# Graph attention's query stores and the first tile's query load on ACT's DMA queue

## The chip, the cores and the metric

The kernel runs on one core of a Trainium2 chip. The metric is the device time of one execution in microseconds (us); of several executions the median is given. PE (TensorE) is the matrix engine, DVE (VectorE), ACT (ScalarE) and POOL (GpSimd) are the others, and SP (SyncE) only issues transfers. SP and ACT each have a DMA queue of their own, in which an engine's transfers stand in program order among its other instructions; POOL issues the indirect transfers. "Tile" is used for a block of 128 nodes.

## The reference

Two layers of a graph network over 1250 nodes with 512 channels and 40000 edges. Each layer adds a graph part, a mixing part and a feed-forward part. The change concerns the graph part of the first layer, an attention in which every edge carries one score per head (8 heads of 64 channels):

```python
xn = _layernorm(x, axis=-1)
x = x + _L0_gnn_ref(xn, edge_index, edge_attr_8, ...) + _L0_mix_ref(xn[None], ...)[0]
...
def _L0_gnn_ref(x, edge_index, att_bias, Wq, bq, Wk, bk, Wv, bv, Wo, bo, ...):
    src = edge_index[0]
    dst = edge_index[1]
    z = _layernorm(x, ln_att_g, ln_att_b)
    q = (z @ Wq.T + bq).reshape(n, H, D)
    k = (z @ Wk.T + bk).reshape(n, H, D)
    v = (z @ Wv.T + bv).reshape(n, H, D)
    s = jnp.einsum('ehd,ehd->eh', q[src], k[dst]) / np.sqrt(D) + att_bias
    m = jax.ops.segment_max(s, src, num_segments=n)
    p = jnp.exp(s - m[src])
    denom = jax.ops.segment_sum(p, src, num_segments=n)
    alpha = p / jnp.where(denom[src] == 0, 1.0, denom[src])
    agg = jax.ops.segment_sum(alpha[:, :, None] * v[dst], src, num_segments=n)
    att = agg.reshape(n, C) @ Wo.T + bo
    x = x + att
    ...
```

After it come the feed-forward part of this layer, then the second layer (a graph convolution, a second mixing part, and a product-key feed-forward).

## The kernel before

The 1250 nodes are padded to 1280: ten tiles of 128. The sparse attention is computed as a dense one. First the 40000 edges are turned into a dense table `adj` in device memory, with a row for each pair (source, destination) and nine columns: eight sums of exp(bias) and a count of edges. Then, for each tile of 128 source nodes, the kernel loads that tile's 128 x 1280 x 9 slab of the table, forms the scores of these nodes against all nodes, takes exp, multiplies by the slab, and multiplies by the values. Nodes without an edge between them have weight 0.

**Edges.** `scatter_edges` (L303) is a generator that handles six columns of edges at a step. A step loads keys (`kr`, L311, on SP's queue apart from the first), compares them on DVE (L325, L335) to merge edges with equal keys, sums their weights on PE (L317), and has POOL add rows into `adj` with an indirect transfer (L351). There are 313 of these, 128 rows each. Other stages call `pump(n)` to run n steps in between, so that the edges are worked off beside the mixing part and the projections.

**Projections** (L605 to L640). `zT` is the normalised, transposed input. For three chunks of columns (512, 512, 256) and for the four blocks m of 128 channels, PE multiplies by Wk and by Wq into PSUM tiles `mm`, of which there are three (`ps_mm`, L75). ACT adds the bias: keys to `kT` in SBUF (L628), queries to `qs` (L632), of which there are three. The queries then go to `q_d` in device memory (L633, twelve stores, on SP's queue). After that, for ten tiles, PE multiplies by Wv (L637) and DVE adds the bias and keeps the values as `gva` (L638). A last `pump` empties the generator.

**Attention** (L645 to L806). The pools of the edges and of the projections are closed before it, so its tiles lie in space that those had. `load_tile(t)` (L654) issues two loads on SP's queue: the slab (L657, 5.9 MB), with added dependencies on the last two batches of scatters, so that all edges are in; and `q`, the queries of this tile's 128 nodes for all channels (L661, 256 KB). `load_tile(0)` is called first; the load of tile t+1 is called within tile t. `count` (L664) has ACT copy the slab's column of counts (`cnt`, L667) and stores it; `mark` (L674) makes DVE's mask `none` of it; `score` (L677) multiplies q by kT on PE (L683); `maxima` (L687) adds the mask on DVE and finds the largest score; then follow exp (L705), the product with the slab (L712), transposes (L722, L723) and the product with the values (L732).

**Order.** Inside the attention loop the order on PE, DVE and ACT is the one written out by hand (`tc.manual_schedule`, L774). Everything before it, the projections and `load_tile(0)`, and all of SP's queue, is ordered by the framework's scheduler when the kernel is built: it puts each engine's instructions into one fixed sequence and gives each the waits that its data and its space need. On the chip each engine then goes through its sequence. In the sequence that SP has here, the loads of q for tiles 0 and 1 come after the ninth query store, then come the last three query stores, and then the slabs of tiles 0 and 1.

Of the kernel before, what the change touches and what calls it, by code (L numbers as in the profile page):

```python
# [22 lines left out]
P = 128  # L23
# [43 lines left out]
def tile_gps_layers(ctx: ExitStack, tc: tile.TileContext, a, out):  # L67
    nc = tc.nc
# [6 lines left out]
    def ps_mm(shape=(P, 512), name="mm"):  # L75
        return psum.tile(list(shape), F32, tag="mm", bufs=3, name=name)
# [4 lines left out]
    def ps_tr(shape=(P, 512), name="tr"):  # L81
        return psum.tile(list(shape), F32, tag="tr", bufs=2, name=name)
# [34 lines left out]
    def col(name, j=0, n=1, p0=0, p1=P):  # L117
        c0 = COLS[name][0] + j
        return cols[p0:p1, c0:c0 + n]

    def rows_bc(pool, src, n, width=C, name="rows", eng=nc.sync):
        t = pool.tile([P, n, width], F32, name=name)
        eng.dma_start(t.rearrange("p r c -> p (r c)"),
                          bass.AP(tensor=src.tensor, offset=src.offset, ap=[[0, P], [1, n * width]]))
        return t

    def load_w(pool, name, kc, n, tag="w", bufs=None, eng=nc.sync):
        t = pool.tile([P, kc, n], F32, tag=tag, name=name, bufs=bufs)
        eng.dma_start(t, a[name].rearrange("(c p) o -> p c o", p=P))
        return t  # L130
# [16 lines left out]
    def norm_stats(pool, x_t, eps, name):  # L147

        st = pool.tile([P, 6], F32, tag="ln_st", name=name + "st")
        nc.vector.bn_stats(st, x_t)  # L150
        mv = pool.tile([P, 2], F32, tag="ln_mv", name=name + "mv")
        nc.vector.bn_aggr(mv, st)
        return mv[:, 0:1], rsqrt(pool, mv[:, 1:2], [P, 1], eps, name)
# [27 lines left out]
    def node_mm(ps, xT, t, w, rows=P):  # L181

        mm(ps[:rows], [(xT[:, c, t * P:t * P + rows], w[:, c, :]) for c in range(xT.shape[1])])
# [7 lines left out]
    def chan_mm(ps, w, m, xT, c0, cn):  # L191

        mm(ps, [(w[:, c, m * P:(m + 1) * P], xT[:, c, c0:c0 + cn]) for c in range(xT.shape[1])])
# [5 lines left out]
    q_d = dram.tile([P, KC, NP], F32, name="q_d")  # L199
# [63 lines left out]
    for c0 in range(0, EC, P):  # L263
        cn = min(P, EC - c0)
# [131 lines left out]
    def pump(n):  # L396
        for _ in range(n):
            next(edges, None)
# [206 lines left out]
    with tc.tile_pool(name="gqkv", bufs=2) as pq:  # L605
        gbv = rows_bc(pq, a["gnn_rows"][0:1], 1, name="gbv")
        wk = load_w(pq, "gnn_WkT", KC, C, bufs=3)
        wq = load_w(pq, "gnn_WqT", KC, C, bufs=3)
        wv = load_w(pq, "gnn_WvT", KC, C, bufs=3)
        zT = pq.tile([P, KC, NP], F32, name="zT", bufs=1)  # L610
        for t in range(NT):
            z = pq.tile([P, C], F32, tag="z", name="z")
            m, r = norm_stats(pq, xn[:, t, :], 1e-5, "lnz")
            b = pq.tile([P, 1], F32, tag="lnzb", name="lnzb")
            nc.vector.tensor_scalar(b, m, r, -1.0, op0=OP.mult, op1=OP.mult)
            nc.scalar.activation(z, xn[:, t, :], AF.Identity, scale=r, bias=b)
            ps = ps_tr((P, KC, P))
            for c in range(KC):
                nc.tensor.transpose(ps[:, c, :], z[:, c * P:(c + 1) * P], ident)
            for c in range(KC):  # L620
                nc.scalar.activation(zT[:, c, t * P:(t + 1) * P], ps[:, c, :], AF.Identity,
                                     scale=col("att_g", c), bias=col("att_b", c))
            nc.scalar.dma_start(xb_d[t * P:(t + 1) * P, :], xn[:, t, :])
        for c0, cn in CHUNKS:
            for m in range(KC):
                ps = ps_mm()
                chan_mm(ps[:, :cn], wk, m, zT, c0, cn)
                nc.scalar.activation(kT[:, m, c0:c0 + cn], ps[:, :cn], AF.Identity, bias=col("gnn_bk", m))  # L628
                ps = ps_mm()
                chan_mm(ps[:, :cn], wq, m, zT, c0, cn)  # L630
                qs = pq.tile([P, 512], F32, tag="qs", name="qs", bufs=3)
                nc.scalar.activation(qs[:, :cn], ps[:, :cn], AF.Identity, bias=col("gnn_bq", m))  # L632
                nc.sync.dma_start(q_d[:, m, c0:c0 + cn], qs[:, :cn])  # L633
                pump(1)
        for t in range(NT):
            ps = ps_mm()
            node_mm(ps, zT, t, wv)  # L637
            nc.vector.tensor_tensor(va[:, t, :], ps, gbv[:, 0, :], op=OP.add)  # L638
            pump(1)
        pump(EC)  # L640
# [5 lines left out]
    with (tc.tile_pool(name="gslab", bufs=2) as pslab, tc.tile_pool(name="gatt", bufs=1) as pa,  # L646
# [7 lines left out]
        def load_tile(t):  # L654

            sl = pslab.tile([P, NP, CH], F32, tag="slab", name="slab")
            ld = nc.sync.dma_start(sl.rearrange("p d c -> p (d c)"), adj_v[t * P:(t + 1) * P, :])  # L657
            for x in scattered[-2] + scattered[-1]:
                tc.add_manual_dep(ld.ins, x.ins.name, SYNC, reason="all edges are in")
            q = pw.tile([P, KC, P], F32, tag="q", name="q")  # L660
            nc.sync.dma_start(q, q_d[:, :, t * P:(t + 1) * P])  # L661
            tiles[t] = [sl, q]

        def count(t):  # L664
# [105 lines left out]
        def stage(i, back):  # L770
            return steps[i - back] if 0 <= i - back < n else None

        load_tile(0)
        with tc.manual_schedule(engines={nc.tensor.engine, nc.vector.engine, nc.scalar.engine}):  # L774
            mark(0, count(0))
            score(*steps[0])
            for i in range(n + 4):
                now, last, turned, gone, done = (stage(i, b) for b in range(5))
                nxt = stage(i, -1)
                if now:  # L780
                    maxima(*now)
                    if now[1] == 0 and now[0] + 1 < NT:
                        load_tile(now[0] + 1)
                if done and done[1] == KC - 1:
                    divide(done[0])
                if turned:
                    turn(*turned, 1)
                    av = values(*turned)
                if nxt:
                    score(*nxt)  # L790
                if now:
                    exponentials(*now)
                    if now[1] == KC - 1 and now[0] + 1 < NT:
                        cnt = count(now[0] + 1)
                if turned:
                    keep(*turned, av)
                if last:
                    weigh(*last)
                    turn(*last, 0)
                if now and now[1] == KC - 1 and now[0] + 1 < NT:  # L800
                    mark(now[0] + 1, cnt)
                if last and last[1] == KC - 1:
                    divisors(last[0])
                if gone and gone[1] == KC - 1:
                    spread_divisors(gone[0])
# [1195 lines left out]
```

## Time and profile before

| | us |
|---|---|
| median of 3 runs | 2412.15 (2410.34 to 2412.55) |
| the profiled execution | 2407.95 |
| its span, first to last instruction | 2406.0 |
| POOL's scatters (L351), first to last start | 194.3 to 787.3 |
| query projections (L632), first to last start | 666.4 to 737.5 |
| query stores (L633, SP's queue), first to last issue | 667.1 to 792.9 |
| loads of q (L661, SP's queue), first to last issue | 790.3 to 1089.4 |
| loads of the slabs (L657), first to last issue | 795.6 to 1108.4 |
| first copy of counts (L667), ACT | starts 812.3 |
| attention's scores (L683), first to last start | 794.2 to 1160.1 |

PE is busy for 1978.7 us of the span (82%), DVE for 1510.5 (63%), ACT for 809.2 (34%) and POOL for 695.8 (29%). These shares are means over stages with different limits. Times in views of the trace count from the span's start. An entry such as `ACT L632 ... [2.79 <-PE even L317]` says that ACT was idle for 2.79 us before this work, and that the idle time ended with PE's work on the tile `even` at L317. `PEclk` is the clock that was granted to PE, as a share of full speed.

### The profile page before, as it was taken

What the parts mean: (1) busy time and instruction counts of PE and PEld (TensorE: products, weight loads), DVE (VectorE), ACT (ScalarE), POOL (GpSimd) and SP (SyncE); (2) the same over time, 40 slices, a digit from 0 to 9 for tenths busy, and PEclk for the clock granted to TensorE, in tenths of its full rate; (3) what the DMA queues carried; (4) which work ended last, traced back from release to release, by engine and by line L of the source; (5) the groups of instructions that cost most, each with busy time, mean ns of one, the idle gap of its engine ahead of it and who ended that gap; (6) DMA issues with size and microseconds to landing.
All of it is one profiled execution on the core that took longest, in us unless ns stands there. A gap on an engine that the chain in (4) does not pass through costs nothing.

```text
span 2406.0 us, 29781 instructions
## 1 busy us (share of the span) xinstructions
PE 1978.7 (82%) x10588; PEld 1178.0 (49%) x10588; DVE 1510.5 (63%) x4838; ACT 809.2 (34%) x1529; POOL 695.8 (29%) x448
## 2 busy tenths in 40 slices
PE   0767698885498499999899999999999999978943
PEld 0335475552244266666544546667445445555521
DVE  3716958879961399999651446655222142589997
ACT  0100011110230277677441156665111132244653
POOL 2006888888888100000000000000000000036665
PEclk9987698986599699999999999999899999989975
DMA  9998565434542665665431200000300101000000
GB/s 352 367 418 237 111 127 113 86 61 88 136 72 10 238 224 186 232 217 193 139 119 35 68 3 1 1 1 29 136 27 27 35 7 64 22 22 10 10 9 17
DMA packets 134385, 255.79 MB, mean 106 GB/s; under 512 B 51805, under 2 KB 90134, under 8 KB 132572
## 3 DMA queue, kind: packets, MB, share of 16 engines
q1 hardware_dynamic: 81840, 233.85, 26.3%
q0 software_dynamic: 46512, 8.02, 7.0%
q10 hardware_dynamic: 5884, 12.03, 1.4%
q8 instruction: 83, 1.36, 0.2%
q14 instruction: 66, 0.54, 0.1%
HBM read 161.05 MB, written 92.80 MB: 106 GB/s over the span
## 4 chain that ended last, share of the span: by engine, by line
PE 46%; DVE 12%; ACT 6%; DMA 1%; issue 1%; SPq 0%; POOL 0%; ACTq 0%; DVEq 0%
PE mm L179 21%; PE one L732 4%; PE sc L683 3%; ACT wT L723 3%; PE ag L1385 2%; PE sc L1064 2%; PE one L722 2%; PE av L1118 2%; PE one L1105 2%; DVE sc L1745 2%; DVE ix L1686 1%; DVE ix L1695 1%; DVE rest L1698 1%; DVE v L1692 1%; DVE v L1694 1%
## 5 line engine op out<-in xcount | busy, mean ns | idle before, releaser
L351 POOL DMA_INDIRECT adj<-tot,idx x313 | 499.0, 1594 | 276.0 <-DMA kr<-key_d 180.5
L712 DVE SCALAR_TENSOR_TENSOR ex<-ex,slab 128x1280 f32<-128x1280 f32 x80 | 197.3, 2510 | 0.2 <-issue 0.2
L325 DVE SCALAR_TENSOR_TENSOR eq<-kr,key,upto 128x128 bf16<-128x128 f32 (+2 forms) x313 | 145.0, 474 | 66.6 <-DMA kr<-key_d 41.0
L1316 DVE SCALAR_TENSOR_TENSOR X<-mm,gate,X 128x512 f32<-128x512 f32 x80 | 60.0, 750 | 199.1 <-PE mm L179 199.0
L335 DVE TENSOR_SCALAR_CACHE_REDUCE eqx<-kr,key 128x384 bf16<-128x384 f32 (+1 forms) x312 | 175.3, 598 | 0.0
L1254 POOL MEMSET padded<- 128x128 f32 x3 | 0.5, 205 | 541.0 <-DVE faT L1139 541.0
L722 PE MATMUL one<-ident,ex 128*128 128x128 f32 x800 | 126.2, 286 | 25.2 <-ACT wT L723 19.9
L723 ACT COPY wT<-one 128x512 f32<-128x512 f32 (+1 forms) x240 | 116.1, 517 | 90.2 <-PE one L722 85.5
L179 PE MATMUL mm<-w,hT 128*128 128x512 f32 (+1 forms) x320 | 143.9, 601 | 0.0
L179 PE MATMUL mm<-faT,w 128*128 128x512 f32 (+1 forms) x384 | 141.8, 523 | 0.7 <-ACT bs L1138 0.7
L683 PE MATMUL sc<-kT,q 64*128 64x512 f32 (+1 forms) x480 | 103.7, 556 | 42.0 <-DMA q<-q_d 22.4
L693 DVE CUSTOM_DVE_ANT_0 ex<-sc,none 128x1280 f32<-128x1280 f32 x80 | 115.8, 1486 | 11.3 <-PE sc L683 10.0
L722 PEld LDWEIGHTS one<-ident,ex 128*128 128x128 f32 x800 | 84.5, 141 | 68.4 <-ACT wT L723 48.8
L1078 DVE CUSTOM_DVE_ANT_0 ex<-sc,cmask 128x512 f32<-128x512 f32 (+3 forms) x144 | 72.9, 560 | 69.2 <-PE sc L1064 69.1
L317 PEld LDWEIGHTS <-eq 128*128 128x128 bf16 x625 | 42.9, 102 | 133.6 <-DVE eq L325 88.7
L179 PEld LDWEIGHTS mm<-faT,w 128*128 128x128 f32 x384 | 74.6, 195 | 67.4 <-issue 66.1
L705 ACT ACTIVATE ex<-ex,low 128x1280 f32<-128x1280 f32 x80 | 104.7, 1360 | 6.0 <-DVE low L698 6.0
L669 POOL DMA_DIRECT2D deg_d<-cnt x10 | 8.5, 846 | 338.9 <-ACT attT L739 312.6
L732 PE MATMUL one<-wT,gva 128*64 128x128 f32 x1600 | 101.3, 284 | 3.4 <-ACT wT L723 1.5
L1310 ACT ACTIVATE hT<-mm,cols 128x512 f32<-128x512 f32 (+1 forms) x48 | 29.0, 608 | 218.4 <-PE mm L179 218.4
L732 PEld LDWEIGHTS one<-wT,gva 128*64 128x64 f32 x1600 | 91.6, 143 | 13.4 <-ACT wT L723 13.4
L179 PEld LDWEIGHTS mm<-w,hT 128*128 128x128 f32 (+1 forms) x320 | 60.8, 191 | 75.5 <-issue 75.5
(493 smaller groups left out, 4094.2 us busy)
## 6 DMA issues: line engine op xcount, KB each, us to landing
adj<-zrow SPq DMA_DIRECT2D x4, 14400.0 KB
slab<-adj SPq DMA_DIRECT2D x10, 5760.0 KB
kr<-key_d SPq DMA_DIRECT2D x50, 576.0 KB
cnt_d<-cnt SPq DMA_DIRECT2D x10, 640.0 KB
deg_d<-cnt POOLq DMA_DIRECT2D x10, 640.0 KB
adjT<-cnt_d SPq DMA_DIRECT2D x5, 1280.0 KB
adj<-tot,idx POOLq DMA_INDIRECT x313
fw<-in_L_ffn_W SPq DMA_DIRECT2D x8, 512.0 KB
```

Of the source, the lines that this page charges most:

```text
L179: nc.tensor.matmul(ps, lhsT=l, rhs=r, start=i == 0, stop=i == len(pairs) - 1)
L325: nc.vector.scalar_tensor_tensor(eq[:, :n], kr[:, k0 * P:k0 * P + n], key[:, c0 + c:c0 + c + 1], upto[:, B - 1 - c:, :].rearrange("p c x - ...
L335: nc.vector.tensor_scalar(eq[:, :n * P], kr[:, k0 * P:(k0 + n) * P], key[:, c0 + c:c0 + c + 1], None, op0=OP.is_equal, op1=OP.add, accum_o ...
L351: st = nc.gpsimd.indirect_dma_start(out=adj, out_offset=bass.IndirectOffsetOnAxis(ap=idx[:, c:c + 1], axis=0), in_=tot[:, c, :], in_offset ...
L683: nc.tensor.matmul(sc[e][:, d0:d0 + dn], lhsT=q[half(e), m, :], rhs=kT[half(e), m, d0:d0 + dn], start=True, stop=True)
L693: nc.vector.tensor_tensor_reduce(out=ex, in0=sc[e][:, :NP], in1=none, scale=-0.125, scalar=-LOWEST, op0=OP.add, op1=OP.min, accum_out=low[ ...
L705: nc.scalar.activation(exs[e], exs[e], AF.Exp, bias=low[:, e:e + 1], scale=-1.0)
L712: nc.vector.scalar_tensor_tensor(exs[e], exs[e], 1.0, sl[:, :, hd], op0=OP.mult, op1=OP.mult, accum_out=den[:, hd:hd + 1])
L722: nc.tensor.transpose(ps[:, k, :], weights[t, m][e][:, (d0 + k) * P:(d0 + k + 1) * P], ident)
L723: nc.scalar.copy(wT[:, d0:d0 + dn, :], ps[:, :dn])
L732: nc.tensor.matmul(av[half(e), 0, :], lhsT=va[:, d, hd * D:(hd + 1) * D], rhs=turned[e][:, d, :], start=d == 0, stop=d == NT - 1)
L1078: nc.vector.tensor_tensor_reduce(out=exs[e][:, d0:d0 + dn], in0=sc[k][e][:, :dn], in1=cmask[:, NP - n + d0:NP - n + d0 + dn], scale=-0.125 ...
```

## The change

The twelve stores of the queries are issued from ACT in place of SP. Of the ten loads of q, the one for tile 0 is issued from ACT, and the other nine from SP as before. What is stored and loaded stays as it was, and so do the tiles and their numbers of buffers.

```diff
@@ -630,7 +630,7 @@
                 chan_mm(ps[:, :cn], wq, m, zT, c0, cn)
                 qs = pq.tile([P, 512], F32, tag="qs", name="qs", bufs=3)
                 nc.scalar.activation(qs[:, :cn], ps[:, :cn], AF.Identity, bias=col("gnn_bq", m))
-                nc.sync.dma_start(q_d[:, m, c0:c0 + cn], qs[:, :cn])
+                nc.scalar.dma_start(q_d[:, m, c0:c0 + cn], qs[:, :cn])
                 pump(1)
@@ -658,7 +658,9 @@
             q = pw.tile([P, KC, P], F32, tag="q", name="q")
-            nc.sync.dma_start(q, q_d[:, :, t * P:(t + 1) * P])
+
+            queue = nc.sync if t else nc.scalar
+            queue.dma_start(q, q_d[:, :, t * P:(t + 1) * P])
             tiles[t] = [sl, q]
```

## The prediction

> **What bounds the kernel now.** I read the stage around the change. First came the order of time of SP's queue, because both moved transfers stand on it now.
>
> ```profile
> 723.27 4.60 SPq L633 DMA_DIRECT2D q_d<-qs  x2
> 790.34 1.29 SPq L661 DMA_DIRECT2D q<-q_d  x2
> 791.74 1.50 SPq L633 DMA_DIRECT2D q_d<-qs  x3
> 795.60 0.80 SPq L657 DMA_DIRECT2D slab<-adj  x2
> ```
>
> Columns: start, length, engine, line, tiles. SP stops after the ninth of twelve query stores at 727.9 and issues nothing until 790.34. What holds it is the load of q for tiles 0 and 1, which the scheduler put ahead of the last three stores. The chain that ended last, in order of time, shows what ends that wait and what follows:
>
> ```profile
> 787.28 2.93 DMA adj<-tot,idx
> 790.34 0.62 SPq L661
> ...
> 792.87 2.59 DMA q_d<-qs
> 795.60 16.62 DMA slab<-adj
> 812.32 2.46 ACT cnt L667
> 814.80 0.84 DVE none L675
> ```
>
> The q load is freed by the landing of the last edge scatter (787.28 + 2.93 = 790.21), not by its own data: its buffer lies where the edge tiles were. Then come three late stores, their landing, and the slab. So 5.3 us of the chain (790.34 to 795.60) belong to the transfers that the change moves. Next, the order of time of PE, ACT and DVE, for what runs while POOL scatters:
>
> ```profile
> 730.37 1.89 PE L179 MATMUL mm<-zT,gnn_WkT 128*128 128x256 f32 x8
> 732.09 1.89 PE L179 MATMUL mm<-zT,gnn_WqT 128*128 128x256 f32 x8
> 733.82 1.89 PE L179 MATMUL mm<-zT,gnn_WkT 128*128 128x256 f32 x8
> 735.54 1.89 PE L179 MATMUL mm<-zT,gnn_WqT 128*128 128x256 f32 x8
> 737.27 34.50 PE L179 MATMUL mm<-gnn_WvT,zT 128*128 128x512 f32 x80
> 794.21 4.64 PE L683 MATMUL sc<-kT,q 64*128 64x512 f32 x12 [22.44 <-DMA q<-q_d]
> ```
>
> ```profile
> 728.84 0.47 ACT L628 ACTIVATE kT<-mm,cols 128x256 f32<-128x256 f32 x1 [1.32 <-PE mm L179]
> 730.62 0.47 ACT L632 ACTIVATE qs<-mm,cols 128x256 f32<-128x256 f32 x1 [1.30 <-PE mm L179]
> ```
>
> ```profile
> 771.81 0.69 DVE L638 TENSOR_TENSOR gva<-mm,gbv 128x512 f32<-128x512 f32 x1 [2.74 <-PE mm L179]
> ```
>
> The last key and query products and all 34.5 us of value products run under the scatters. The values are done at 772.50, 17.8 us before the scatters land: that is their cover.
>
> **The change, part by part.** Line numbers are those of before. *Order.* Compared as built, PE, DVE and POOL keep their orders; only ACT and SP change. SP loses twelve stores and one load. On ACT each store stands behind its qs. But the scheduler puts the load of tile 0's q after the kT of (last chunk, m=1), ahead of the qs of m=1, of kT and qs of m=2 and 3, and of three stores. Its list of waits is the one it had on SP: all eight lanes of the scatters, up to the 313th.
>
> *Nine stores before that point.* Each costs ACT 0.33 us (the ten xb_d stores on ACT's queue, median 332 ns): 9 x 0.33 = 3.0 us. Between 677 and 728 ACT idles 1.4 to 4.2 us ahead of each L628 and L632, waiting for PE, so I take 0. Even uncovered, 3.0 us fit into the 17.8 us of cover. On SP the key loads (L311) no longer stand behind stores, which waited up to 7.8 us for qs. That gains 0: POOL issues scatters every 1.85 us, with no gap over 0.6 us between 640 and 740, until 788.8, while DVE has no scatter work left after 740. A loss has no source either.
>
> *The wait on ACT.* ACT reaches the load after 728.84 + 0.47 = 729.3 and stands there until 790.34, when SP was let through with the same list. That an ACT computation stands behind a waiting transfer of its own queue is shown at the kernel's start:
>
> ```profile
> 29.91 2.75 DVE L282 TENSOR_TENSOR wgt<-wgt,mx 128x2504 f32<-128x2504 f32 x1
> ```
>
> ```profile
> 53.80 0.51 ACTq L269 DMA_DIRECT2D key_d<-kt  x1
> ...
> 55.63 1.28 ACT L283 ACT_TABLE_LOAD   x1 [55.63 <-DMA key_d<-kt]
> ```
>
> The exponential L283 had its input at 32.7, but its table load came only after the transfers ahead of it, at 55.6. [...]
>
> *What is queued behind it.* Products go into three PSUM buffers (mm). kT m=1 gives its buffer back at 729.3; q m=1, k m=2 and q m=2 then fill all three, and PE stops at 734.0, before k m=3. Behind it in PE's order stand q m=3, the ten value tiles and the scores. DVE's adds (L638) wait for PE, and the slab load waits for the tenth add (in before's list too), because the slab takes space of this stage. The cover is gone, and the new path is:
> - 790.34: load issued on ACT, 0.61 us (att_d on ACT's queue, 607 ns; SP's q loads 529 to 624): 790.95.
> - qs m=1: 0.05 + 0.47: 791.47; PE starts k m=3 at 791.5, where before it was 733.82, so PE is 57.7 us late.
> - PE needs 771.77 - 733.82 = 37.95 us for the rest at full clock. After 57 us of idling it starts at the low clock. Two restarts show how long that lasts (PEclk is the number before the last two):
>
> ```profile
> 796.00:798.00 2.00, 2.00 (x8) 0.98 (x6) 0.00 (x0) 0.00 (x0) 0.00 (x0) 0.50 1.17 369
> 798.00:800.00 2.00, 0.84 (x4) 0.12 (x2) 0.00 (x0) 0.00 (x0) 0.00 (x0) 0.69 0.86 369
> ...
> 822.60:824.00 1.40, 0.73 (x2) 0.06 (x1) 1.40 (x3) 0.28 (x1) 0.00 (x0) 0.81 1.92 549
> ```
>
> A mean of 0.69 over 798 to 800 means 0.50 for 62% of it and 1.00 for the rest, so after the start at 794.21 the clock rises at 799.2 (5.0 us); in the same way 0.81 puts the rise after the start at 817.34 at 823.1 (5.8 us). At half rate that loses 2.5 to 2.9 us; I take 2.7. Bounds: 0 with no low clock, 38 if it never rose. [...]
> - The last add then ends at 772.50 + 57.7 + 2.7 = 832.9. The slab issues 0.14 later (795.60 against the landing at 795.46): 833.0. Three stores of 0.33 us on ACT and the last two evacuations fall under PE's 3.4 us per tile: 0; uncovered, +1 to +2.
> - q stores land long before (last qs near 799, +2.6): no cost. Tile 0's scores follow the values on a warm PE and end near 834.6, ahead of the mask, as before.
>
> Sum: 833.0 - 795.60 = **+37.4 us**. From cnt on, nothing differs but the date. The profiled span 2406.0 becomes 2443.4, its execution 2407.95 becomes 2445.4. The median of the runs lies 4.2 us above that execution: 2412.15 + 37.4 = **2449.6 us**.
>
> **The rivals.**
> - *Faster or equal: the load doesn't hold ACT.* Then all stores land before 745, and the slab issues once tile 1's q is issued: 790.34 + 0.62 + 0.05 = 791.0, which is 4.6 us earlier: 2407.6. It decides if ACT is let go before about 752: PE then is at most 791.0 - 772.5 = 18.5 us late. For it: the chain's 5.3 us are real. Against it: the list of waits, and SP's 56.8 us longest wait at L661 put down to the scatter. 3 in 100.
> - *Half the loss: the slab doesn't need the values.* It issues after the last store lands, near 802, so the scores bind: 771.8 + 60.4 + 2.4 (12 warm matmuls) = 834.6 against the first maximum at 815.78, +18.8, less 2.8 for the second scores, warm (2.4 for 5.2): +16.0, 2428. Against it: the tenth add on the slab's list. 4 in 100.
> - *Double loss: the clock stays low.* +34.7 + 38 = +72.7, 2485. For it: 0.50 to 0.6 in idle stretches. Against it: both restarts. 2 in 100.
> - *No effect:* ACT's wait ends near 757, so that PE is 23.1 us late and the 4.6 us are just given back. 2 in 100.
>
> **How the numbers follow.** The forecast has 89 in 100. Its own terms span +34.7 (no low clock) to +39.6 (clock 2.9, ACT +2), so 2447 to 2452; for the sizes read from one execution I widen this to 2441 to 2456, which leaves the rivals and some of the forecast out. About 0.2% (4.8 us) is what a measurement of this kernel can tell from no change; the first rival's -4.6 lies at that edge. Faster 0.02, same 0.03, slower 0.95.
>
> **What would show it.** ACT idle from 729 to 790 ahead of a qs; PE idle from 734 to 791.5, its releaser ACT's L632; value products from about 798 to 832; the slab issued near 833 and cnt near 849.6; from there every group as long as before. Wrong if the slab issues before 815, if the values end before 790, or if the stage after cnt changes its length.

## The result and the profile after

The changed kernel took 2447.14 us (median of 4 runs, 2445.60 to 2450.06), the kernel before, on the same chip beside it, 2411.24 (4 runs, 2410.02 to 2412.55). The ratio is 1.0157, with a 95% interval of 1.014 to 1.0173: 36 us slower by the medians. The profiled execution took 2447.29 us with a span of 2445.5, against 2407.95 and 2406.0 before.

SP's queue in order of time, to set beside the four lines of before (start, length, engine, line, tiles):

```profile
655.61 60.68 SPq L311 DMA_DIRECT2D kr<-key_d  x6
791.65 0.62 SPq L663 DMA_DIRECT2D q<-q_d  x1
834.17 0.81 SPq L657 DMA_DIRECT2D slab<-adj  x2
```

No store of queries is left there. But the slab, which was issued 4.0 us after the last q load's issue had ended, is now issued 41.9 us after the end of the one that remains. ACT in the same order of time shows where this begins:

```profile
727.48 0.47 ACT L628 ACTIVATE kT<-mm,cols 128x256 f32<-128x256 f32 x1 [1.36 <-PE mm L179]
791.61 0.61 ACTq L663 DMA_DIRECT2D q<-q_d  x1
792.33 0.47 ACT L632 ACTIVATE qs<-mm,cols 128x256 f32<-128x256 f32 x1 [64.37 <-DMA adj<-tot,idx]
792.83 0.34 ACTq L633 DMA_DIRECT2D q_d<-qs  x1
```

Between 727.95 and 791.61 ACT does nothing. The bias behind the load (L632) names the edge scatters as what ended its idle time, though it needs nothing of theirs: its operand, PE's product of 727.28, has lain in PSUM since 729.2. The load that stands ahead of it needs them. PE in order of time shows what became of the cover:

```profile
730.73 1.89 PE L179 MATMUL mm<-zT,gnn_WqT 128*128 128x256 f32 x8
792.85 3.78 PE L179 MATMUL mm<-zT,gnn_WkT 128*128 128x256 f32 x8 [60.23 <-ACT qs L632]
796.43 2.61 PE L179 MATMUL mm<-zT,gnn_WqT 128*128 128x256 f32 x8
798.87 34.50 PE L179 MATMUL mm<-gnn_WvT,zT 128*128 128x512 f32 x80
834.15 2.42 PE L685 MATMUL sc<-kT,q 64*128 64x512 f32 x12 [0.78 <-DVE gva L638]
855.93 6.04 PE L685 MATMUL sc<-kT,q 64*128 64x512 f32 x12 [19.36 <-DVE low L695]
862.73 6.04 PE L685 MATMUL sc<-kT,q 64*128 64x512 f32 x12 [0.76 <-DVE low L695]
```

The 80 value products take 34.50 us, as they did before, but they start at 798.87 where they started at 737.27. All of PE's remaining work has slid from under the scatters to behind them. The chain that ended last (start, length, what) joins the pieces:

```profile
788.57 2.90 DMA adj<-tot,idx
...
791.61 0.61 ACTq L663
...
792.33 0.48 ACT qs L632
...
792.85 40.53 PE mm L179 x96
...
833.40 0.70 DVE gva L638
...
834.17 16.64 DMA slab<-adj
...
850.91 2.46 ACT cnt L669
```

Where before two q loads and three late stores stood between the last landing and the slab, 5.39 us, there is now a bias, 40.53 us of PE and an add: 834.17 - (788.57 + 2.90) = 42.70 us. The difference is 37.3 us. The scatters themselves landed 1.26 us later in this execution, and the stretch from the copy of counts to the span's end is 1594.6 us against 1593.7. Together: 37.3 + 1.3 + 0.9 = 39.5, the difference of the spans.

Stretches of time of the same kernel (length; busy time of PE, PE's weight loads, DVE, ACT and POOL; then PE's granted clock, the share of the DMA engines, GB/s):

```profile
734.00:790.00 56.00, 0.00 (x0) 0.00 (x0) 0.00 (x0) 0.00 (x0) 46.86 (x31) 0.52 0.25 3
796.00:798.00 2.00, 2.00 (x6) 1.62 (x5) 0.00 (x0) 0.47 (x1) 0.00 (x0) 0.53 0.04 12
798.00:800.00 2.00, 2.00 (x8) 1.33 (x7) 0.00 (x0) 0.47 (x1) 0.00 (x0) 1.00 0.00 0
857.00:859.00 2.00, 2.00 (x6) 1.42 (x6) 0.45 (x3) 1.48 (x2) 0.00 (x0) 0.50 0.95 410
869.00:871.00 2.00, 2.00 (x10) 1.55 (x8) 2.00 (x5) 0.88 (x2) 0.00 (x0) 0.50 0.00 0
873.00:875.00 2.00, 1.69 (x24) 1.32 (x24) 2.00 (x3) 1.84 (x4) 0.00 (x0) 1.00 0.00 0
```

From 734 to 790 only POOL works. PE restarts at half clock at 792.85 (0.50 over 790 to 796). A mean of 0.53 over 796 to 798 puts the rise at 797.9, 5.0 us after the start. At the second scores (855.93) the clock stays at half until about 873, for 17 us, though PE is busy nearly throughout (13.25 of the 14 us from 857 to 871). Before, the rise there came after 5.8 us.

### The profile page after: what moved, and what is told of

Same layout as the page of the kernel before. It is cut to its first block, busy times and chain, and to the rows that moved or that the text cites. A ratio compares the mean times of both kernels' runs of the same rounds, so it can differ in the third digit from the quotient of the medians.

```text
span 2445.5 us, 29782 instructions
## 1 busy us (share of the span) xinstructions
PE 1981.9 (81%) x10588; PEld 1182.7 (48%) x10588; DVE 1510.5 (62%) x4838; ACT 809.0 (33%) x1529; POOL 695.1 (28%) x448
## 3 DMA queue, kind: packets, MB, share of 16 engines
q8 instruction: 84, 1.38, 0.2%
## 4 chain that ended last, share of the span: by engine, by line
PE 47%; DVE 12%; ACT 6%; DMA 2%; issue 1%; SPq 0%; ACTq 0%; DVEq 0%
PE mm L179 22%; PE sc L685 4%; PE one L734 4%; ACT wT L725 3%; PE one L724 2%; PE ag L1387 2%; PE sc L1066 2%; PE av L1120 2%; PE one L1107 2%; DVE sc L1747 2%; DVE ix L1688 1%; DVE ix L1697 1%; DVE rest L1700 1%; DVE v L1694 1%; DVE v L1696 1%
## 5 line engine op out<-in xcount | busy, mean ns | idle before, releaser
L695 DVE CUSTOM_DVE_ANT_0 ex<-sc,none 128x1280 f32<-128x1280 f32 x80 | 115.7, 1484 | 15.1 <-PE sc L685 13.9
```

The costliest lines, as they stand in the source:

```text
L695: nc.vector.tensor_tensor_reduce(out=ex, in0=sc[e][:, :NP], in1=none, scale=-0.125, scalar=-LOWEST, op0=OP.add, op1=OP.min, accum_out=low[ ...
```

## The experiments

The kernels ran in four groups, each beside runs of the kernel before. The theory: the load of tile 0's q stands in ACT's sequence between two biases, waits there for the scatters, and holds ACT, through it PSUM, PE and the values, and through them the slab. The rival theories: the twelve stores on ACT are what costs; or the loss is as long as the hold, whatever stands behind it; or it comes from PE's clock. In the table, "to slab" and "to cnt" count from the landing of the last scatter to the issue of the first slab and to the first copy of counts; "rest" is from there to the end of the span. These three come from one profile each. The medians of the kernel before were 2411.24 us beside the change, 2409.70 beside the next three and load_behind_queries, 2411.66 beside load_behind_keys, q_own_place and the first two with PE kept busy, and 2408.35 beside queries_own_pool and the two twins. The last column is the ratio of the times to the kernel before, with its 95% interval.

| run | to slab | to cnt | rest | median us | ratio |
|---|---|---|---|---|---|
| the kernel before | 5.39 | 22.11 | 1593.7 | 2411.24 | 1 |
| the change | 42.70 | 59.44 | 1594.6 | 2447.14 | 1.0157 [1.014, 1.0173] |
| changed_again | 42.34 | 59.07 | 1597.7 | 2448.30 | 1.0156 [1.014, 1.0173] |
| load_only | 42.30 | 59.55 | 1590.6 | 2443.94 | 1.0143 [1.0126, 1.0161] |
| stores_only | 1.71 | 20.69 | 1591.6 | 2407.84 | 0.999 [0.998, 1.0001] |
| load_behind_queries | 1.03 | 18.24 | 1594.0 | 2406.69 | 0.9982 [0.997, 0.9993] |
| load_behind_queries_twin | 1.03 | 18.17 | 1596.2 | 2405.68 | 0.9984 [0.997, 0.9999] |
| load_behind_keys | 32.35 | 49.03 | 1594.3 | 2436.17 | 1.011 [1.0091, 1.013] |
| q_own_place | 1.70 | 20.68 | 1598.8 | 2411.54 | 1.0006 [0.9996, 1.0016] |
| queries_own_pool | 0.13 | 16.58 | 1599.3 | 2407.85 | 0.9992 [0.9981, 1.0003] |
| changed_pe_kept_busy | 43.10 | 59.59 | 1591.8 | 2445.68 | 1.0142 [1.0126, 1.0159] |
| load_behind_queries_pe_kept_busy | 1.03 | 18.35 | 1597.7 | 2403.57 | 0.9972 [0.9959, 0.9985] |
| pe_kept_busy_twin | 1.03 | 18.34 | 1592.9 | 2404.09 | 0.9979 [0.9969, 0.9989] |

### The two halves of the change, each alone

The stores alone (stores_only); the load goes back to SP:

```diff
-            queue = nc.sync if t else nc.scalar
-            queue.dma_start(q, q_d[:, :, t * P:(t + 1) * P])
+            nc.sync.dma_start(q, q_d[:, :, t * P:(t + 1) * P])
```

> Only the twelve query stores go through ACT's queue; all ten loads of q stay on SP's. Theory (the load of tile 0's q holds ACT behind the scatters, and the values lose their cover): without the load on ACT nothing holds it; the values end near 772 as before, SP issues two loads of q once the scatters land and the slab right behind them, about 1.4 us after the landing in place of 5.4 us: 3.5 to 5 us faster than before, near 2407.5 with before at 2411.5. Rival (the stores themselves cost ACT its time, or their landing is late): still slower than before, by most of the 36 us.

The load alone (load_only); the stores go back to SP:

```diff
-                nc.scalar.dma_start(q_d[:, m, c0:c0 + cn], qs[:, :cn])
+                nc.sync.dma_start(q_d[:, m, c0:c0 + cn], qs[:, :cn])
```

> Only tile 0's load of q goes through ACT's queue; the stores stay on SP's. Theory: ACT is held from about 728 to 791 ahead of the query bias of block 1 of the last chunk, exactly as in the changed kernel; PE idles about 57 us, the slab is issued about 42.5 us after the last scatter lands: +34 to +39 us over before. Rival (the stores on ACT are what costs): within 5 us of before.

The change once more, beside them (changed_again, no edit):

> The changed kernel once more, for a second profile. Theory: up to the slab's issue everything stands at the same distance from the last scatter's landing (slab issued 42.7 us after it, within 0.5); the stretch from the first copy of counts to the end is 1594.6 us in the first profile against 1593.7 before, made of 5 us more in attention and 4 us less after it, both from when the granted PE clock goes down and up; if that is so, these two differ by some us from profile to profile of the same kernel. If they come out equal to 1 us, the 5 us belong to the change.

The load alone brings the whole loss: 1.0143, with the change at 1.0156 in the same group and intervals that overlap. PE in order of time, load_only:

```profile
730.32 1.89 PE L179 MATMUL mm<-zT,gnn_WqT 128*128 128x256 f32 x8
793.15 3.78 PE L179 MATMUL mm<-zT,gnn_WkT 128*128 128x256 f32 x8 [60.94 <-ACT qs L632]
```

It is the same stop, with the same releaser, and without a single store on ACT. The stores alone cost nothing: the ratio is 0.999, and PE goes on to the value products as in the kernel before. PE's line for them, then SP's queue there:

```profile
736.38 34.50 PE L179 MATMUL mm<-gnn_WvT,zT 128*128 128x512 f32 x80
```

```profile
656.11 60.65 SPq L311 DMA_DIRECT2D kr<-key_d  x6
789.48 1.29 SPq L661 DMA_DIRECT2D q<-q_d  x2
791.01 0.89 SPq L657 DMA_DIRECT2D slab<-adj  x2
```

The three late stores are gone from the path, and the slab issues 1.7 us after the landing in place of 5.4. Of these 3.7 us only 1.4 arrive at the copy of counts (20.69 against 22.11), because the slab's transfer, right behind two q loads, took 18.87 us and not 16.62. The time fell by 1.9 us between the medians, less than the 3.5 to 5 us expected, and its interval includes 1.

changed_again repeats the distance from landing to slab (42.34 against 42.70). Behind it the two profiles of the change differ: from the copy of counts to the last product with the slab 365.2 against 367.0 us, and from there to the end 1232.5 against 1227.6. So the 4 us less at the end, which the first profile has against the kernel before (1231.7), don't belong to the change.

### The place of the load in ACT's order

The next edit is the change, with one dependency more: the load of tile 0's q stands behind the last query bias.

```diff
-                nc.scalar.activation(qs[:, :cn], ps[:, :cn], AF.Identity, bias=col("gnn_bq", m))
+                query = nc.scalar.activation(qs[:, :cn], ps[:, :cn], AF.Identity, bias=col("gnn_bq", m))
...
+            tc.add_manual_dep(ql.ins, query.ins.name, SYNC, reason="behind the queries")
```

> The changed kernel with one added dependency: tile 0's load of q stands behind ACT's last query bias. It still waits for the last scatter on ACT's queue. Theory (what counts is what is queued behind the wait): ACT waits as long, but with nothing of the projections behind it; values end near 772, slab issued about 0.8 us after the landing: 4 to 5.5 us faster than before, near 2407. Rival (a waiting transfer on ACT's queue costs by itself, or ACT's queue is slower for this load): slower than before by 5 us or more.

In order of time on ACT:

```profile
737.21 0.33 ACTq L633 DMA_DIRECT2D q_d<-qs  x1
789.56 0.61 ACTq L661 DMA_DIRECT2D q<-q_d  x1
807.66 2.46 ACT L668 COPY cnt<-slab 128x1280 f32<-128x1280 f32 x1 [70.48 <-DMA slab<-adj]
```

The load still stands on ACT's queue and still waits for the scatters. Now nothing is behind it that PE needs, and the 36 us are gone; the kernel is 0.18% faster than before (3.0 us between the medians, 4.3 by the ratio, where 4 to 5.5 were expected). So neither ACT's queue as such nor the wait as such costs, but what the scheduler put behind it.

The same with the dependency on the last key bias lets a single query bias (m = 3) and its store stand behind the load:

```diff
+                key_m = nc.scalar.activation(kT[:, m, c0:c0 + cn], ps[:, :cn], AF.Identity, bias=col("gnn_bk", m))
...
+            tc.add_manual_dep(ql.ins, key_m.ins.name, SYNC, reason="behind the keys")
```

> The changed kernel with tile 0's load of q moved further down on ACT: behind the key bias of block 3 of the last chunk, so that one query bias (and its store) instead of five biases stands behind the wait. Theory (PE stops when the three PSUM buffers are full, and the slab waits for the tenth value tile): the last query product holds one buffer, the values of tiles 0 and 1 take the other two and get done, and PE stops only ahead of the third value tile, near 744; eight value tiles (27.5 us) are left for after the landing instead of ten and two products (38 us). With 1.6 us from landing to PE's start and 2.5 to 2.9 us lost at the low clock the slab is issued about 32.5 us after the landing in place of 42.5: +25 to +30 us over before. Rivals: the slab waits only for the last store (then about +0 to +5), or ACT's wait as such costs the 36 us (then +36).

ACT at the load, then PE, in order of time:

```profile
792.73 0.47 ACT L632 ACTIVATE qs<-mm,cols 128x256 f32<-128x256 f32 x1 [57.59 <-DMA adj<-tot,idx]
```

```profile
734.46 1.89 PE L179 MATMUL mm<-zT,gnn_WqT 128*128 128x256 f32 x8
736.18 7.03 PE L179 MATMUL mm<-gnn_WvT,zT 128*128 128x512 f32 x16
793.25 30.09 PE L179 MATMUL mm<-gnn_WvT,zT 128*128 128x512 f32 x64 [50.04 <-ACT qs L632]
```

The query product and two value tiles fill the three PSUM buffers, and PE stops at 743. One bias held back is enough. ACT stood nearly as long (57.6 us, against 64.4 in the change), but the slab comes 10.35 us earlier than in the change (32.35 against 42.70), which is what PE had done less to do after its restart: 40.53 - 30.11 = 10.4 (both from the chain of waits). The price is thus the work that loses its cover, not the length of the hold. It was 24.5 us by the medians, just short of what was expected, and 26.5 by the ratio, inside it.

### Another place in SBUF

Here the load doesn't wait for the scatters, because its tile doesn't lie where theirs were: tile 0's queries get a buffer in the pool of kT and gva.

```diff
+    q0 = pg.tile([P, KC, P], F32, name="q0")
...
+            q = pw.tile([P, KC, P], F32, tag="q", name="q") if t else q0
```

> The changed kernel with a buffer for tile 0's q of its own, in the pool of the keys and values, so that this load needs no space of the edges' stage. Theory (the wait is one for space, not for data): the load on ACT now waits only until the first chunk's four stores have landed, some 2 to 3 us near 690, and not for a scatter; PE doesn't stop, the values end near 772, the slab is issued about 1 us after the landing, tile 0's scores run right after the values near 772 instead of at 793: 4 to 5.5 us faster than before. Rival (the wait is for the queries' data, or the load on ACT's queue is late by itself): slower than before.

The hold is gone, and the whole +36 us with it; the load is issued long before the scatters land:

```profile
692.03 0.60 ACTq L662 DMA_DIRECT2D q<-q_d  x1
```

But the expected gain over the kernel before didn't come. The chain:

```profile
786.38 2.96 DMA adj<-tot,idx
...
789.52 0.62 SPq L662
...
790.20 0.61 SPq L662
...
791.04 18.88 DMA slab<-adj
```

With tile 0 out of the way, tiles 1 and 2 take the two shared buffers, which still lie in the edges' space. So two q loads stand between landing and slab, and the slab again takes 18.9 us. From landing to cnt it is the time of stores_only (20.68 against 20.69). The expectation had counted the earlier issue and not the slower transfer. Nor do the 1.4 us gained up to cnt last: behind it the profile has 1598.8 us against 1593.7.

So both buffers of q went into that pool, after which no early load of q waits for scatters:

```diff
-            q = pw.tile([P, KC, P], F32, tag="q", name="q")
+            q = pg.tile([P, KC, P], F32, tag="q", name="q", bufs=2)
```

> Both buffers of q lie in the pool that lives through the projections, so the loads for tiles 0 and 1 wait for their data alone and are done long before the edges are in; the slab then stands alone on SP's queue at the last landing. Theory (each q load that stands ahead of the slab in one queue costs issue and transfer time; one more of them cost 2.4 us between the runs with one and with two): the slab issues 0.1 to 0.3 us after the landing and takes 16.5 to 16.8 us, the copy of counts starts 16.7 to 17.2 us after the landing (22.1 in the kernel before, 20.7 with two loads ahead, 18.2 with one), and the time is 4.5 to 5.5 us below the kernel before, near 2406. Rival (the slab is slow because it starts right behind the scatters): it takes 18.9 us here too, the copy starts 19.1 us after the landing, 3 us below the kernel before.

Its chain:

```profile
787.75 2.90 DMA adj<-tot,idx
790.78 16.35 DMA slab<-adj
807.23 2.46 ACT cnt L667
```

The first half of the expectation holds: the slab issues 0.13 us after the landing, its transfer alone takes 16.35 us, and cnt comes 16.58 us after the landing, 5.5 earlier than before (both a little under what was expected). So the 18.9 us don't come from starting right behind the scatters, but go with the two loads right ahead of the slab on its queue. The second half missed: the time is 0.9992 [0.9981, 1.0003] of the kernel before, no gain that can be told from none. In the profile the rest took 1599.3 us against 1593.7, and that 5.6 us is the whole gain.

### PE's clock

What is the long low clock at the second scores worth? The change, with 22 products more behind tile 0's scores, whose results nothing uses:

```diff
+            busy = ps_one()
+            for _ in range(22):
+                nc.tensor.matmul(busy.rearrange("p k c -> p (k c)"), lhsT=ident, rhs=kT[:, 0, :512], start=True, stop=True)
```

> The changed kernel with 22 matmuls of no use (18.9 us at the value products' pace) on PE between tile 0's first and second scores, where PE idles 19.4 us waiting for the slab. Theory (the 5 us that attention lost in the first profile of the changed kernel come from the granted PE clock, which stayed at 0.50 for 17 us after that idle stretch against 5.8 before): the clock is 1.00 at the second scores, the stretch from the first copy of counts to the end of the last product with the slab falls from 367 to 357 to 361 us, and the run is 3 to 8 us faster than the changed kernel. Rival (the 5 us come from transfers or from order): that stretch stays at 362 us or more, run within 2 us of the changed kernel.

Two of its stretches of time, in the columns explained above:

```profile
857.00:859.00 2.00, 1.82 (x4) 0.29 (x2) 2.00 (x3) 0.00 (x0) 0.00 (x0) 1.00 0.99 415
859.00:861.00 2.00, 1.83 (x9) 0.88 (x10) 0.28 (x3) 1.65 (x2) 0.00 (x0) 1.00 1.01 433
```

The clock is full there, and from the copy of counts to the last slab product (the end of the line that L712 was) the profile has 360.3 us, against 367.0 and 365.2 in the two profiles of the change. But the median fell by 1.5 to 2.6 us (2445.68 against 2447.14 and 2448.30), less than expected, and the ratios to the kernel before (1.0142 against 1.0157 and 1.0156) have intervals that overlap: the gain can't be told from none. The low clock at the second scores explains at most a few us of the loss, and not the 36.

The same with 16 products on top of load_behind_queries:

> The version with the load behind all queries, with 16 such matmuls (13.8 us) in the same place, where PE idles 14.7 us. By the same theory it gains 3 to 6 us over that version, so it is 6 to 10 us faster than before, near 2402 with before at 2410. Rival: the same as without them, near 2406.

It came to 0.9972 of the kernel before, 8.1 us between the medians and 6.8 by the ratio, inside the 6 to 10 us expected against it; but the interval overlaps with that of load_behind_queries (0.9982). So both ran once more, side by side, with twelve executions each:

> The same kernel as in the run with the load behind the queries, beside the next one. From its first runs: 4 to 5 us below the kernel before, a ratio of 0.997 to 0.9993.

> The same with 16 products more on PE, whose results nothing uses, behind tile 0's scores. If a warm clock at the second scores is worth anything to the end, 2 to 6 us below the run without them, a ratio of 0.9955 to 0.9975; if the clock's later dips give it back, within 2 us of it.

With the idle products the time is 2404.09 us, without them 2405.68; the ratios to the kernel before, 0.9979 [0.9969, 0.9989] and 0.9984 [0.997, 0.9999], overlap. The version without them is 2.7 us below the kernel before between the medians and 3.9 by the ratio, a little less than expected. The difference between the two is the second of the two outcomes expected, within 2 us; the products' own worth can't be told from nothing. The version with them is the fastest that was found, 0.2% to 0.3% under the kernel before in both groups.

## Why the prediction was right

The forecast was 2449.6 us, +37.4. Measured were 2447.14 us, +35.9 between the medians and +39.3 between the profiled executions. By its own steps:

- *The load holds ACT from 729.3 until the scatters land.* Held from 727.95 to 791.61. That the load, and nothing else of the change, does this was shown by load_only and stores_only. 64.37 us of ACT's idle time stand ahead of a bias that didn't need the scatters, behind the load that did.
- *Three PSUM buffers fill and PE stops.* PE stopped after q m = 2, as named, at 732.6 (734.0 was named). load_behind_keys moved the stop behind four products more (k and q of m = 3, two value tiles), and the loss fell by their work.
- *PE restarts 1.3 us after the landing (791.5 - 790.21), with 2.7 us lost at the low clock.* It was 1.38 us; from the start of k m = 3 to the first value product there were 6.02 us against 3.45 before (737.27 - 733.82), so 2.57 were lost.
- *The slab follows the last add.* At 834.17, 0.07 us after the add's end (833.40 + 0.70). This excludes the rival in which the slab doesn't need the values.
- *The sum.* From landing to slab +37.3 us, where +37.4 was forecast. That it came so near is in part luck: the second profile of the change has +37.0, and load_only +36.9. The rival with a clock that stays low is out: the value products took 34.50 us.
- *Nine early stores cost nothing.* stores_only shows it (all twelve on ACT, and a ratio of 0.999).
- *Faster, if the load didn't hold ACT, by 4.6 us.* That rival's price was about right, as load_behind_queries shows: the slab 4.4 us earlier after the landing, cnt 3.9 earlier, the time 0.18% less (0.07% to 0.3%), 4.3 us, or 3.0 between the medians.
- *From cnt on nothing differs but the date.* Right in the sum of one profile (1594.6 us against 1593.7), not in the other's (1597.7), and wrong inside both. From cnt to the last slab product the first has 5.0 us more (367.0 against 362.0), and behind it 4.1 us less. The second scores ran at half clock for 17 us in place of 5.8, but that isn't the whole reason for the 5.0: load_behind_queries ran them at half clock for 16.5 us and took 362.5, load_only for 6.0 and took 364.0. The prediction took the length of low clock from two restarts of before as good for every restart.
- *The median lies 4.2 us above the profiled execution.* True of before; the changed kernel's profiled execution lies 0.15 us above its median. The medians' difference is 1.5 us below the forecast and the profiles' 1.9 above; single executions of the changed kernel scatter over 4.5 us (2445.60 to 2450.06), and the interval of the ratio is 34 to 42 us.

## What to carry to other kernels

A transfer that must wait belongs on a queue behind which nothing is urgent, and the place in the built order decides that, not the line in the source: here one load that the scheduler put between two biases cost 36 us, and the same load a few instructions later cost nothing (a ratio of 0.9982). To price such a wait, don't count how long the engine stands, but how much work behind it loses its cover (with 40.53 and 30.11 us of PE's work behind the landing the loss was 36 and 24.5 us, while ACT stood 64.4 and 57.6). And this load waited for what had last lain in the space that it fills (issued at 791.6 us there, at 692.0 from a buffer elsewhere), so look at where a buffer lies before moving its transfer to another queue.

## What the runs showed that was not expected

*The length of the low clock varies while the work doesn't.* At the second scores the same sequence of products, after 19 to 20 us without any, ran at half clock for 17 us in two profiles of the change (873.0 - 855.93 in one) and for 6.0 in load_only. Two stretches of load_only show its rise near 862.3, after a start at 856.32:

```profile
861.00:863.00 2.00, 1.36 (x3) 0.33 (x1) 1.43 (x3) 0.00 (x0) 0.00 (x0) 0.68 1.38 410
863.00:865.00 2.00, 1.59 (x4) 0.59 (x6) 1.75 (x6) 0.29 (x1) 0.00 (x0) 1.00 0.27 110
```

It varies even for one and the same program. load_behind_queries and its twin don't differ, and PE idles for 14.7 and 15.1 us ahead of the second scores. They start at 812.68 in one profile, where the clock rises near 829.2, and at 812.95 in the other, where it rises near 817.9: 16.5 us at half clock against 4.9. First two stretches of load_behind_queries, then two of the twin:

```profile
818.00:820.00 2.00, 1.25 (x3) 0.50 (x2) 2.00 (x3) 0.00 (x0) 0.00 (x0) 0.50 1.39 410
828.00:830.00 2.00, 1.70 (x9) 1.47 (x10) 1.97 (x4) 1.09 (x4) 0.00 (x0) 0.71 0.00 0
```

```profile
816.00:818.00 2.00, 2.00 (x7) 1.06 (x5) 0.00 (x0) 1.15 (x1) 0.00 (x0) 0.53 1.01 433
818.00:820.00 2.00, 0.82 (x4) 0.40 (x3) 1.87 (x3) 0.00 (x0) 0.00 (x0) 1.00 1.51 433
```

So the program alone doesn't set its length. Of the 471 spells of low clock in the 13 traces, 458 last a whole multiple of 3.41 us (71 of 73 in the kernel before and the changed one): 3.4, 6.8, 10.2 and so on to 64.9; the other 13 are the last of each trace, which the end of the record cuts off. In the changed kernel's rows from 857 to 871 the clock is half for 14 us, about four times 3.41, while PE was busy for 13.25 of them. What keeps it low there was not settled.

*Gains of a few us may get lost in that clock.* From the copy of counts on, the 13 profiles do the same work (apart from the idle products), yet take 1590.6 to 1599.3 us; the time at low clock within it goes from 157.0 to 182.1 us (167.8 before, 175.7 in the change's first profile), and the two go together, though loosely (correlation 0.79, some 0.25 us for each us at low clock). The longest rests are those of the two kernels with queries in a place of their own, with 179.9 and 180.3 us at low clock; but load_behind_keys has 181.1 us of it in a rest of only 1594.3. That the clock takes these gains is thus likely and not shown, and whether the two kernels' earlier scores set when it goes low, or single executions fell so, the runs don't tell.

*Loads of q right ahead of the slab cost more than their issue.* The slab took 16.35 us with none, 17.0 to 17.2 with one on its own queue and one on ACT's (four profiles), and 18.9 with two on its own (two profiles), all issued within 1.6 us ahead of it.
